# Weighed rows added to the output one step sooner, scatters issued ahead of the additions, experts' numbers read ahead: a graph layer and a mixture of experts on one core

## The chip, the cores and the metric

The kernel runs on one core of one Trainium2 chip. The metric is the device time of one execution in microseconds; smaller is better. The core has five engines with an instruction queue each: TensorE (PE, with its weight loads shown apart as PEld), VectorE (DVE), ScalarE (ACT), GpSimd (POOL) and SyncE (SP). Each queue works in order. In this kernel SP issues the plain transfers (rows of the profile marked SPq), and POOL issues the indirect ones (gathers, scatters, and additions into rows of the output). A transfer is issued by one instruction and lands some microseconds later; what needs it waits for the landing.

## The reference, cut to what matters

```python
x = x + gnn(layernorm(x), edges)          # 6250 nodes, 512 features, 106250 edges
x = x + ffn(layernorm(x))                 # a mixture of 8 experts, the best 2 for each token

def ffn(t):
    logits = gelu(t @ Wg1 + bg1) @ Wg2 + bg2
    topv, topi = top_k(softmax(logits), 2)
    topv = topv / sum(topv)
    cw = sum(one_hot(topi, 8) * topv[..., None], axis=1)     # a token's weight for each expert
    h = einsum('td,edh->eth', t, W1) + b1                    # 512 -> 256
    h = gelu(ln(h, g1, be1))
    h = einsum('eth,ehg->etg', h, W2) + b2                   # 256 -> 256
    h = gelu(ln(h, g2, be2))
    o = einsum('eth,eho->eto', h, W3) + b3                   # 256 -> 512
    return einsum('te,eto->to', cw, o)
```

The graph part (mean over neighbours, two products, batch norm) comes first and isn't touched by the change. The expert part is computed for the two chosen experts of each token alone.

## The kernel before, in words

**First part.** Until about 1200 us the kernel gathers neighbours' rows and multiplies; until about 1320 us it normalizes the first two groups of tokens.

**Second part.** The 6250 tokens form 49 tiles of 128 in 7 groups of 7 tiles. A tile of tokens is loaded, normalized and added to its input (`token_load`, `token_mul`, `token_add`, `token_sum` and others); `token_sum` (L843) writes the tile into `out` by an SP transfer (L844, called the store below). The routing of a group (`route`) then finds for each token its two experts and a row in `xs_d`, a table in DRAM ordered by expert, and `send` scatters the group's rows there: two indirect transfers of 128 rows per tile of tokens (`row_scatter`, L877).

A job is one tile of 128 rows of `xs_d` that all belong to one expert; 102 jobs run. A job goes through a pipeline of steps written out in `run(s, ...)`: step s works on job s in its first stage, on job s-1 in its second, and so on. With lag in steps: 0 transpose the rows on PE (`job_turn`), 1 first product (`layer`, L1103), 2 normalize (`layer_norm`, L806), 3 transpose and gelu (`layer_turn`), 4 second product, 5 and 6 the same again, 7 third product (`job_product`, L1132), 8 add the bias on DVE (`job_bias`, L1139) and multiply by the tokens' weights on ACT (`job_weigh`, L1143), 9 add the 128 rows into `out` by an indirect accumulating transfer on POOL (`job_out`, L1147, called the addition below). Job p+3 is loaded by SP in step p (`job_load`, L1082: the 512 features into `xe`, and weights and row numbers into `ev`).

**What sets the order.** There is no scheduler here: each engine's queue holds the instructions in the order in which `run` writes them. While tokens are still to be moved, a step also carries one tile of tokens through its own stages, and lists `do` and `late` of the step hold parts of the routing and the scatters. On POOL a step of before therefore reads: the addition of job s-9, then two scatters where the step has any, then the power that turns variances into scales (L797, called the power below). The power of step s ends the step: `shifts` of the next step (DVE L801) waits for it, and the normalizations on ACT wait for that.

**Dependences that matter here.** The additions are chained: each waits for the landing of the one before, because two jobs can hold the same token. Each also waits for the landing of every store of `out` that stands ahead of it in the program, and for its own weighing. A load of `xe` waits for the landing of all scatters ahead of it in the program. `oe` has three buffers, `ev` fourteen, so `job_bias` and the load of `ev` wait for additions of earlier jobs.

An expert's number lies in memory and must be brought into a register of each engine that picks weights by it (`values_load` in `job_turn`, L1088, on PE, DVE and ACT, at the start of the step).

Of the kernel before, what the change touches and what calls it, by code (L numbers as in the profile page):

```python
# [10 lines left out]
I32 = mybir.dt.int32  # L11
# [17 lines left out]
def gnn_moe_kernel(ctx: ExitStack, tc: tile.TileContext, x, src, dst, wlT, b_l, wrT, gamma, beta,  # L29
                   wg1, bg1, wg2, bg2, w1, b1, g1T, be1T, w2, b2, g2T, be2T, w3, b3, out):  # L30
    nc = tc.nc
    N, D = x.shape
    NE = src.shape[0]
    E, _, H = w1.shape
# [33 lines left out]
    NQ = -(-NT // 7)  # L68
# [3 lines left out]
    SLOTS = (2 * N + E * (P - 1)) // P  # L72
# [26 lines left out]
    w3s = const.tile([P, KH, E, D], F32, name="w3s")  # L99
    b1s = const.tile([P, E, H], F32, name="b1s")  # L100
    b2s = const.tile([P, E, H], F32, name="b2s")
    b3s = const.tile([P, E, D], F32, name="b3s")

    gbe = const.tile([P, E, 4, KH], F32, name="gbe")
# [7 lines left out]
    expert = const.tile([P, E], F32, name="expert")  # L112
# [34 lines left out]
    with ExitStack() as gnn:  # L147
        big = gnn.enter_context(tc.tile_pool(name="big", bufs=1))
        edge = gnn.enter_context(tc.tile_pool(name="edge", bufs=1))
        first = ExitStack()  # L150
# [247 lines left out]
        XT, Z = {}, {}  # L398
# [375 lines left out]
    JOBS = {}  # L774
# [293 lines left out]
            send_one(q, j, i)  # L1068


    XE, EV, XT, HN, HT, OE = {}, {}, {}, {}, {}, {}
    PE_, DVE_, ACT_, SP_ = (mybir.EngineType.PE, mybir.EngineType.DVE, mybir.EngineType.Activation,
                            mybir.EngineType.SP)

    def job_load(p):
# [7 lines left out]
            tc.add_to_no_dep_group("full", ld.ins)  # L1083
        XE[p] = xe, ev

    def job_turn(p):
        xe, ev = XE.pop(p)
        e = nc.values_load(JOBS[p][1], engines=[PE_, DVE_, ACT_], min_val=0, max_val=E - 1,  # L1088
                           skip_runtime_bounds_check_because="an expert's number")
        EV[p] = e, ev[:, 0:1].bitcast(I32), ev[:, 1:1 + E][:, ds(e, 1)]  # L1090
        pt = ps.tile([P, KD, P], F32, name="pt", bufs=3)
        for k in range(KD):
            nc.tensor.transpose(pt[:, k, :], xe[:, k * P:(k + 1) * P], ident)
        XT[p] = sb.tile([P, KD, P], F32, name="xT")
        nc.scalar.copy(XT[p], pt)

    def layer(p, i, step):
        e = EV[p][0]
        lhs, w, b, kk = (XT, w1s, b1s, KD) if i == 0 else (HT, w2s, b2s, KH)
        lhs = lhs.pop(p)  # L1100
        pm = ps.tile([P, H], F32, name="pm", bufs=2)
        for k in range(kk):
            nc.tensor.matmul(pm, lhs[:, k, :], w[:, k, ds(e, 1), :].rearrange("p o h -> p (o h)"),  # L1103
                             start=(k == 0), stop=(k == kk - 1))
        hn = sb.tile([P, H], F32, name=f"hn{i}", bufs=3)
        nc.vector.tensor_add(hn, pm, b[:, ds(e, 1), :].rearrange("p o h -> p (o h)"))  # L1106
        HN[p] = hn, step.stats(1 + i, hn)

    def layer_norm(p):
# [3 lines left out]
    def layer_turn(p, i):  # L1113

        e = EV[p][0]
        hn, _ = HN.pop(p)
        hT = sb.tile([P, KH, P], F32, name=f"hT{i}")
        pt = ps.tile([P, KD, P], F32, name="pt", bufs=3)
        for k in range(KH):
            nc.tensor.transpose(pt[:, k, :], hn[:, k * P:(k + 1) * P], ident)  # L1120
        for k in range(KH):
            gb = gbe[:, ds(e, 1), :, k].rearrange("p o j -> p (o j)")
            nc.scalar.activation(hT[:, k, :], pt[:, k, :], AF.Gelu,  # L1123
                                 bias=gb[:, 2 * i + 1:2 * i + 2], scale=gb[:, 2 * i:2 * i + 1])
        HT[p] = hT

    def job_product(p):
        e = EV[p][0]
        hT = HT.pop(p)
        po = ps.tile([P, D], F32, name="po")  # L1130
        for k in range(KH):
            nc.tensor.matmul(po, hT[:, k, :], w3s[:, k, ds(e, 1), :].rearrange("p o h -> p (o h)"),  # L1132
                             start=(k == 0), stop=(k == KH - 1))
        OE[p] = po

    def job_bias(p):
        e = EV[p][0]
        oe = sb.tile([P, D], F32, name="oe", bufs=3)
        nc.vector.tensor_add(oe, OE[p], b3s[:, ds(e, 1), :].rearrange("p o h -> p (o h)"))  # L1139
        OE[p] = oe  # L1140

    def job_weigh(p):
        nc.scalar.mul(OE[p], OE[p], EV[p][2])  # L1143

    def job_out(p):
        _, to, _ = EV.pop(p)
        st = nc.gpsimd.indirect_dma_start(  # L1147
            out=out[:, :], out_offset=bass.IndirectOffsetOnAxis(ap=to[:, 0:1], axis=0),
            in_=OE.pop(p), in_offset=None, bounds_check=N - 1, oob_is_err=False, compute_op=OP.add)
        tc.add_to_no_dep_group("added", st.ins)  # L1150
# [7 lines left out]
    def at(lag):  # L1158
        return seq[-1 - lag] if lag < len(seq) else None

    def enter():

        nonlocal entered
        seq.append(flat[entered] if entered < let_in else None)
        entered += seq[-1] is not None
# [34 lines left out]

    MOST = SLOTS - 3

    def run(s, prev, lo, hi, moves=False, do=(), late=()):


        def on(lag):
            return lo <= s - lag < hi

        step = Step()
        if moves:  # L1210
            enter()
            if at(0):
                token_load(*at(0))
        loads(min(s + 4, hi))
        if on(0):
            job_turn(s)
        for i, lag in ((0, 3), (1, 6)):
            if on(lag):
                layer_turn(s - lag, i)
        if on(9):  # L1220
            job_out(s - 9)
        if on(8):
            job_bias(s - 8)
        if moves:
            if at(5):
                token_logits(*at(5))
            if at(1):
                token_mul(*at(1))
        tprev.shifts()
        prev.shifts()  # L1230
        if moves:
            if at(1):
                token_add(*at(1))
            if at(2):
                token_sum(*at(2), step)
        for lag in (2, 5):
            if on(lag):
                layer_norm(s - lag)
        if moves and at(3) and at(3) != normed_one:
            token_norm(*at(3))  # L1240
        if on(8):
            job_weigh(s - 8)
        if moves and at(1):
            token_shift(*at(1))
        for f in do:
            f()
        if on(1):
            layer(s - 1, 0, step)
        if on(4):
            layer(s - 4, 1, step)  # L1250
        if on(7):
            job_product(s - 7)
        for f in late:
            f()
        if moves and at(3):
            token_turn(*at(3))
        if moves and at(4):
            token_gate(*at(4))
        step.scales()
        return step  # L1260
# [20 lines left out]
    with tc.manual_schedule():  # L1281
# [26 lines left out]
        n = n0 + n1  # L1308
# [25 lines left out]
        prev = Step()  # L1334
        for q in range(NQ):
            lo = done[q - 1] if q else 0
            n = done[q] - lo
            do = [[] for _ in range(n)]
            late = [[] for _ in range(n)]
            if q + 1 < NQ:  # L1340

                g = len(groups[q + 1])

                def put(where, i, f, *args):
                    where[min(i, n - 1)].append(lambda: f(*args))


                r = int(q == 1)
                if q:
                    put(do, r, begin, q + 1)  # L1350
                    for where, i in ((do, 0), (do, 0), (late, 0), (do, 1), (do, 1), (do, 2), (do, 3)):
                        put(where, r + i, part, q + 1)
                    a, b, end = r + 4, r + 10, (11, 12)
                    if q + 2 == NQ:
                        a, b = 3, 9
                else:
                    for where, i in ((late, 0), (do, 1), (do, 1), (do, 2), (do, 2)):
                        put(where, i, part, 1)
                    a, b, end = 3, 5, (4, 5)
                for j in range(g):  # L1360
                    put(do, a + j * (b + 1 - a) // g, send, q + 1, j)
                if q + 2 < NQ:
                    put(do, end[0], part, q + 1)
                else:
                    for i in (4, 5, 6):
                        put(do, i, part, q + 1)
                    for e in range(E):
                        put(do, 10 + (3 * e + 1) // E, free_rows, e)
                put(do, end[1], listed_all, q + 1)
            for i in range(min(n, MOST - lo)):  # L1370
                if i == (3 if q else 0) and q + 2 < NQ:
                    let(q + 2)
                prev = run(lo + i, prev, 0, MOST, q + 1 < NQ, do[i], late[i])
                if q == NQ - 1 and i == 6:
                    flag = nc.values_load(more[0:1, 0:1], skip_runtime_bounds_check_because="it is 0 or 1")
        for s in range(MOST, MOST + 10):
            prev = run(s, prev, 0, MOST)
    with tc.If(flag > 0), tc.manual_schedule():
        prev = Step()
        for s in range(MOST, SLOTS + 10):  # L1380
            prev = run(s, prev, MOST, SLOTS)


# [35 lines left out]
```

## Time and profile before

| what | us |
|---|---|
| median of 14 runs | 2041.21 (2035.87 to 2047.15) |
| the profiled execution: its time | 2038.17 |
| the profiled execution: its span | 2036.4 |
| the additions L1147: 102 | 165.7 busy, 1624 ns each |
| the scatters L877 from tokens: 98 | 101.4 busy, 1034 ns each |
| the powers L797: 121 | 107.1 busy, 885 ns each |
| PE, DVE, ACT, POOL busy over the span | 1863.6, 1062.9, 646.6, 1224.3 |

The span is that of one profiled execution, from its first to its last instruction; 1.8 us lie around it. The profiled execution is 3.0 us quicker than the median. Times in timelines count from the start of the span. An engine's row gives the start, the duration, the source line and, in square brackets, how long the engine stood idle before it and what the profile takes for the end of that wait. Where the engine named there had long been done, it was something else, often the landing of a transfer.

### The profile page before, as it was taken

Reading aid. Unit: us, or ns where it says so; the run is one execution under the profiler, and the core shown is the slowest. Engines: PE = TensorE matmul, PEld = TensorE weight load, DVE = VectorE, ACT = ScalarE, POOL = GpSimd, SP = SyncE. Lnnn points to the kernel's source line nnn. Section 1 sums busy time; section 2 is a strip of 40 time slices with the busy share of each in tenths; the row PEclk is TensorE's granted clock in tenths of the full one; section 3 lists DMA queues with packets and bytes.
Section 4 is the critical chain, followed back from the end, with each engine's and each line's share of the span. In section 5 each row is a group of like instructions: output and inputs, shape, how many; then the busy total and the mean of one; then the engine's idle time right before and its main releaser. Section 6 shows DMA issues by size and latency. Waiting matters only on the chain. (4 is left out here: it accounts for less than half of the span.)

```text
span 2036.4 us, 24258 instructions
## 1 busy us (share of the span) xinstructions
PE 1863.6 (92%) x6268; PEld 1029.6 (51%) x6268; DVE 1062.9 (52%) x2374; ACT 646.6 (32%) x1263; POOL 1224.3 (60%) x1236
## 2 busy tenths in 40 slices
PE   6878999999999999999999995679989998999993
PEld 2433444444444444444444443456667676666761
DVE  5652434334443444344344426768777777765551
ACT  3420101101010001011010114456666667656662
POOL 1427777777777777777777751445554546474343
PEclk9988999999999999999999997689999999999997
DMA  7968878778788888889888755646676767565532
GB/s 250 302 211 274 255 239 256 240 239 250 242 242 267 267 260 275 260 273 312 269 273 278 242 181 182 224 154 174 170 199 153 199 143 195 115 155 121 95 59 35
DMA packets 197875, 434.12 MB, mean 213 GB/s; under 512 B 47172, under 2 KB 53326, under 8 KB 197314
## 3 DMA queue, kind: packets, MB, share of 16 engines
q0 software_dynamic: 91040, 274.90, 48.2%
q1 hardware_dynamic: 106294, 156.70, 23.4%
q8 instruction: 56, 0.92, 0.2%
q10 hardware_dynamic: 396, 0.87, 0.1%
q14 instruction: 89, 0.73, 0.1%
HBM read 331.22 MB, written 104.20 MB: 214 GB/s over the span
## 5 line engine op out<-in xcount | busy, mean ns | idle before, releaser
L636 POOL DMA_INDIRECT xg<-xn_d,scol x832 | 794.8, 955 | 260.7 <-issue 124.2
L643 PE MATMUL pa<-xg,sel 128*128 128x512 f32 x1664 | 789.6, 597 | 20.3 <-issue 18.5
L643 PEld LDWEIGHTS pa<-xg,sel 128*128 128x128 f32 x1664 | 306.6, 191 | 365.0 <-issue 348.3
L1147 POOL DMA_INDIRECT out<-oe,ev x102 | 165.7, 1624 | 203.0 <-ACT hT L1123 52.2
L1103 PE MATMUL pm<-w1s,xT 128*128 x816 | 202.5, 392 | 8.5 <-DVE hn L1106 8.3
L1132 PE MATMUL po<-w3s,hT 128*128 x408 | 197.6, 607 | 11.4 <-DVE oe L1139 11.4
L528 ACT ACTIVATE sq<-dt 128x512 f32<-128x512 f32 x49 | 29.5, 602 | 557.5 <-DVE dt L526 281.5
L562 DVE TENSOR_REDUCE ss<-sel 128x128 f32<-128x2304 f32 x49 | 200.5, 4091 | 0.3 <-issue 0.2
L432 PE MATMUL ph<-wl,xT 128*128 128x512 f32 x392 | 199.8, 592 | 0.7 <-ACT xT L427 0.7
L797 POOL TENSOR_TENSOR mv<-mv,mhalf 128x2 f32<-128x2 f32 (+2 forms) x121 | 107.1, 885 | 151.3 <-DVE mv L796 149.2
L1103 PEld LDWEIGHTS pm<-w1s,xT 128*128 128x128 f32 x816 | 150.2, 194 | 28.1 <-DVE hn L1106 10.5
L1123 ACT ACTIVATE hT<-pt,gbe 128x128 f32<-128x128 f32 x408 | 153.9, 461 | 1.6 <-PE pt L1120 1.6
L806 ACT ACTIVATE hn<-hn,mv 128x256 f32<-128x256 f32 x204 | 112.0, 599 | 132.4 <-DVE mv L801 132.1
L507 DVE TENSOR_SCALAR rc<-pt 128x1 f32<-128x1 f32 x49 | 7.7, 158 | 272.2 <-PE pt L586 272.2
L556 DVE TENSOR_TENSOR sel<-jrow_p,dcol 128x2304 f32<-128x2304 f32 x49 | 124.4, 2539 | 0.0
L877 POOL DMA_INDIRECT xs_d<-t,pos x98 | 101.4, 1034 | 36.6 <-issue 25.0
L432 PEld LDWEIGHTS ph<-wl,xT 128*128 128x128 f32 x392 | 74.4, 190 | 94.2 <-issue 93.2
L526 DVE TENSOR_TENSOR dt<-ph,shift 128x512 f32<-128x512 f32 x25 | 17.3, 692 | 192.4 <-PE ph L432 192.4
L1132 PEld LDWEIGHTS po<-w3s,hT 128*128 128x128 f32 x408 | 77.0, 193 | 75.0 <-issue 53.0
L567 ACT ACTIVATE ag<-pa,rc 128x512 f32<-128x512 f32 x49 | 33.7, 687 | 249.0 <-PE pa L643 249.0
L524 DVE TENSOR_TENSOR dt<-ph,xo 128x512 f32<-128x512 f32 x24 | 16.6, 691 | 182.3 <-PE ph L432 182.3
L1103 PE MATMUL pm<-w2s,hT 128*128 x408 | 106.3, 383 | 0.0
(302 smaller groups left out, 2205.3 us busy)
## 6 DMA issues: line engine op xcount, KB each, us to landing
xe<-xs_d SPq DMA_DIRECT2D x102, 256.0 KB
xg<-xn_d,scol POOLq DMA_INDIRECT x832, 3.9
d_d<-dt SPq DMA_DIRECT2D x49, 256.0 KB
dt<-d_d SPq DMA_DIRECT2D x49, 256.0 KB
xt<-in_x SPq DMA_DIRECT2D x24, 512.0 KB
xn_d<-xt SPq DMA_DIRECT2D x24, 512.0 KB
xy<-y_d SPq DMA_DIRECT2D x48, 256.0 KB
xt<-in_x SPq DMA_DIRECT2D x48, 256.0 KB
```

The source lines that it names most:

```text
L432: nc.tensor.matmul(p, xT[:, k, :], w[:, k, :], start=start and k == 0, stop=stop and k == KD - 1)
L556: nc.vector.tensor_tensor(SEL[t], jrow_p[:, None, :].to_broadcast([P, KS, P]), dcol[:, t // TG, (t % TG) * KS:(t % TG + 1) * KS, None].to_ ...
L562: nc.vector.tensor_reduce(ss, SEL[t].rearrange("p k j -> p j k"), AX.X, OP.add)
L636: nc.gpsimd.indirect_dma_start(out=xg, out_offset=None, in_=xn_d[:, :], in_offset=bass.IndirectOffsetOnAxis(ap=scol[:, t // TG, c:c + 1], ...
L643: nc.tensor.matmul(PA[t], SEL[t][:, k, :], xg, start=(k == 0), stop=(k == last))
L797: nc.gpsimd.tensor_tensor(self.part[:, :, 1], self.part[:, :, 1], mhalf[:, :hi - lo], op=OP.pow)
L806: nc.scalar.activation(out_, in_, AF.Identity, bias=scale_shift[1], scale=scale_shift[0])
L877: st = nc.gpsimd.indirect_dma_start(out=xs_d.rearrange("n p c -> (n p) c"), out_offset=bass.IndirectOffsetOnAxis(ap=at, axis=0), in_=rows_ ...
L1103: nc.tensor.matmul(pm, lhs[:, k, :], w[:, k, ds(e, 1), :].rearrange("p o h -> p (o h)"), start=(k == 0), stop=(k == kk - 1))
L1123: nc.scalar.activation(hT[:, k, :], pt[:, k, :], AF.Gelu, bias=gb[:, 2 * i + 1:2 * i + 2], scale=gb[:, 2 * i:2 * i + 1])
L1132: nc.tensor.matmul(po, hT[:, k, :], w3s[:, k, ds(e, 1), :].rearrange("p o h -> p (o h)"), start=(k == 0), stop=(k == KH - 1))
L1147: st = nc.gpsimd.indirect_dma_start(out=out[:, :], out_offset=bass.IndirectOffsetOnAxis(ap=to[:, 0:1], axis=0), in_=OE.pop(p), in_offset=N ...
```

## The change

Three things are moved; no arithmetic is changed.

1. `job_out` is called in the step in which its job is weighed (lag 8), right after `job_weigh`, and no longer at the start of the next step (lag 9). The loops over the last steps are shorter by one.
2. The scatters (`send`, `free_rows`) go into a list `first`, which `run` works off before `job_bias`, and no longer into `do`. On POOL a step now reads: scatters, the addition of job s-8, the power. In the stretch of the last group of scatters they are spread over steps 4 to 9 and no longer 3 to 9, so that step 4 has those of two tiles.
3. The experts' numbers for job s+1 are read in step s: on DVE behind `job_bias`, on ACT behind the weighing and the `do` list, on PE behind the first product. Each engine now has a register of its own.

```diff
+    def number(p, engine):
+        if p in JOBS and engine not in NUMBER.setdefault(p, {}):
+            NUMBER[p][engine] = nc.values_load(JOBS[p][1], engines=[engine], min_val=0, max_val=E - 1,
+                                               skip_runtime_bounds_check_because="an expert's number")
     def job_turn(p):
         xe, ev = XE.pop(p)
-        e = nc.values_load(JOBS[p][1], engines=[PE_, DVE_, ACT_], min_val=0, max_val=E - 1,
-                           skip_runtime_bounds_check_because="an expert's number")
+        for engine in (PE_, DVE_, ACT_):
+            number(p, engine)
+        e = NUMBER.pop(p)
...
-    def run(s, prev, lo, hi, moves=False, do=(), late=()):
+    def run(s, prev, lo, hi, moves=False, first=(), do=(), late=()):
...
-        if on(9):
-            job_out(s - 9)
+        for f in first:
+            f()
         if on(8):
             job_bias(s - 8)
+        if on(-1):
+            number(s + 1, DVE_)
         if moves:
...
         if on(8):
             job_weigh(s - 8)
+        if on(8):
+            job_out(s - 8)
         if moves and at(1):
             token_shift(*at(1))
         for f in do:
             f()
+        if on(-1):
+            number(s + 1, ACT_)
         if on(1):
             layer(s - 1, 0, step)
+        if on(-1):
+            number(s + 1, PE_)
         if on(4):
...
                     if q + 2 == NQ:
-                        a, b = 3, 9
+                        a, b = 4, 9
...
-                    put(do, a + j * (b + 1 - a) // g, send, q + 1, j)
+                    put(first, a + j * (b + 1 - a) // g, send, q + 1, j)
...
-                        put(do, 10 + (3 * e + 1) // E, free_rows, e)
+                        put(first, 10 + (3 * e + 1) // E, free_rows, e)
...
-        for s in range(MOST, MOST + 10):
+        for s in range(MOST, MOST + 9):
```

More of the change, by code (lines that the diff above doesn't have):

```diff
@@ L1068, in send @@
             send_one(q, j, i)
-    XE, EV, XT, HN, HT, OE = {}, {}, {}, {}, {}, {}
+    XE, EV, XT, HN, HT, OE, NUMBER = {}, {}, {}, {}, {}, {}, {}
     PE_, DVE_, ACT_, SP_ = (mybir.EngineType.PE, mybir.EngineType.DVE, mybir.EngineType.Activation,
@@ L1084, in job_load @@
         XE[p] = xe, ev
+    def number(p, engine):
+        if p in JOBS and engine not in NUMBER.setdefault(p, {}):
+            NUMBER[p][engine] = nc.values_load(JOBS[p][1], engines=[engine], min_val=0, max_val=E - 1,
+                                               skip_runtime_bounds_check_because="an expert's number")
     def job_turn(p):
         xe, ev = XE.pop(p)
-        e = nc.values_load(JOBS[p][1], engines=[PE_, DVE_, ACT_], min_val=0, max_val=E - 1,
-                           skip_runtime_bounds_check_because="an expert's number")
-        EV[p] = e, ev[:, 0:1].bitcast(I32), ev[:, 1:1 + E][:, ds(e, 1)]
+        for engine in (PE_, DVE_, ACT_):
+            number(p, engine)
+        e = NUMBER.pop(p)
+        EV[p] = e, ev[:, 0:1].bitcast(I32), ev[:, 1:1 + E][:, ds(e[ACT_], 1)]
         pt = ps.tile([P, KD, P], F32, name="pt", bufs=3)
@@ L1102, in layer @@
         for k in range(kk):
-            nc.tensor.matmul(pm, lhs[:, k, :], w[:, k, ds(e, 1), :].rearrange("p o h -> p (o h)"),
+            nc.tensor.matmul(pm, lhs[:, k, :], w[:, k, ds(e[PE_], 1), :].rearrange("p o h -> p (o h)"),
                              start=(k == 0), stop=(k == kk - 1))
         hn = sb.tile([P, H], F32, name=f"hn{i}", bufs=3)
-        nc.vector.tensor_add(hn, pm, b[:, ds(e, 1), :].rearrange("p o h -> p (o h)"))
+        nc.vector.tensor_add(hn, pm, b[:, ds(e[DVE_], 1), :].rearrange("p o h -> p (o h)"))
         HN[p] = hn, step.stats(1 + i, hn)
@@ L1121, in layer_turn @@
         for k in range(KH):
-            gb = gbe[:, ds(e, 1), :, k].rearrange("p o j -> p (o j)")
+            gb = gbe[:, ds(e[ACT_], 1), :, k].rearrange("p o j -> p (o j)")
             nc.scalar.activation(hT[:, k, :], pt[:, k, :], AF.Gelu,
@@ L1131, in job_product @@
         for k in range(KH):
-            nc.tensor.matmul(po, hT[:, k, :], w3s[:, k, ds(e, 1), :].rearrange("p o h -> p (o h)"),
+            nc.tensor.matmul(po, hT[:, k, :], w3s[:, k, ds(e[PE_], 1), :].rearrange("p o h -> p (o h)"),
                              start=(k == 0), stop=(k == KH - 1))
@@ L1138, in job_bias @@
         oe = sb.tile([P, D], F32, name="oe", bufs=3)
-        nc.vector.tensor_add(oe, OE[p], b3s[:, ds(e, 1), :].rearrange("p o h -> p (o h)"))
+        nc.vector.tensor_add(oe, OE[p], b3s[:, ds(e[DVE_], 1), :].rearrange("p o h -> p (o h)"))
         OE[p] = oe
@@ L1337, in gnn_moe_kernel @@
             n = done[q] - lo
+            first = [[] for _ in range(n)]
             do = [[] for _ in range(n)]
@@ L1372, in gnn_moe_kernel @@
                     let(q + 2)
-                prev = run(lo + i, prev, 0, MOST, q + 1 < NQ, do[i], late[i])
+                prev = run(lo + i, prev, 0, MOST, q + 1 < NQ, first[i], do[i], late[i])
                 if q == NQ - 1 and i == 6:
                     flag = nc.values_load(more[0:1, 0:1], skip_runtime_bounds_check_because="it is 0 or 1")
-        for s in range(MOST, MOST + 10):
+        for s in range(MOST, MOST + 9):
             prev = run(s, prev, 0, MOST)
@@ L1379, in gnn_moe_kernel @@
         prev = Step()
-        for s in range(MOST, SLOTS + 10):
+        for s in range(MOST, SLOTS + 9):
             prev = run(s, prev, MOST, SLOTS)
```

## The prediction

> **What bounds the kernel now.** The page comes first. The chain that ended last holds only the final addition, so it says nothing of the rest. PE is busy for 92% of the span, the other engines for 32 to 60%:
>
> ```profile
> PE 1863.6 (92%) x6268; PEld 1029.6 (51%) x6268; DVE 1062.9 (52%) x2374; ACT 646.6 (32%) x1263; POOL 1224.3 (60%) x1236
> ```
>
> That is a mean over stages, and the change touches only those in which additions run (1379 us to the end). So I cut that part into stretches with the view of windows. Columns: window, length, then PE, PEld, DVE, ACT, POOL busy, granted clock, DMA share, GB/s.
>
> ```profile
> 1492.77:1539.19 46.42, 41.07 (x199) 28.81 (x198) 33.81 (x83) 33.55 (x68) 28.02 (x24) 0.96 0.77 217
> 1548.02:1591.13 43.11, 42.99 (x203) 30.84 (x204) 32.62 (x126) 28.08 (x61) 19.85 (x17) 1.00 0.64 137
> 1842.00:1888.00 46.00, 46.00 (x210) 34.54 (x209) 25.60 (x77) 32.00 (x72) 19.12 (x17) 0.98 0.59 111
> 1888.00:1965.00 77.00, 73.73 (x328) 52.07 (x328) 40.82 (x120) 47.81 (x107) 30.08 (x26) 1.00 0.51 87
> ```
>
> The second and third are filled by PE (42.99 of 43.11, 46.00 of 46.00): there only a later end of the additions can matter. The first is one of four spans of six steps that store a token tile; in it PE stands for 5.35 us though no engine is full. What holds it is read from the timelines of POOL, SP's queue and DVE, in that order (start, duration, line; in brackets the idle time before):
>
> ```profile
> 1500.25 1.77 POOL L1147 DMA_INDIRECT out<-oe,ev  x1 [1.55 <-DMA out<-xt]
> ...
> 1503.64 0.99 POOL L877 DMA_INDIRECT xs_d<-t,pos  x1 [0.31 <-issue]
> 1504.78 0.88 POOL L797 TENSOR_TENSOR mv<-mv,mhalf 128x3 f32<-128x3 f32 x1
> 1508.30 1.62 POOL L1147 DMA_INDIRECT out<-oe,ev  x1 [2.64 <-ACT t L806]
> ...
> 1512.53 0.94 POOL L797 TENSOR_TENSOR mv<-mv,mhalf 128x3 f32<-128x3 f32 x1
> 1518.31 1.62 POOL L1147 DMA_INDIRECT out<-oe,ev  x1 [4.84 <-ACT gts L866]
> ```
>
> ```profile
> 1502.19 0.34 SPq L1082 DMA_DIRECT2D xe<-xs_d  x1
> ...
> 1503.24 0.44 SPq L844 DMA_DIRECT2D out<-xt  x1
> ...
> 1509.63 0.34 SPq L1082 DMA_DIRECT2D xe<-xs_d  x1
> ...
> 1510.68 0.43 SPq L844 DMA_DIRECT2D out<-xt  x1
> ```
>
> ```profile
> 1513.50 0.17 DVE L801 SCALAR_TENSOR_TENSOR mv<-mv 128x3 f32<-128x3 f32 x1 [0.99 <-POOL mv L797]
> ...
> 1514.18 0.68 DVE L843 SCALAR_TENSOR_TENSOR xt<-dt,xt 128x512 f32<-128x512 f32 x1
> ```
>
> POOL stands ahead of the additions for 1.55, 2.64 and 4.84 us, and the power that ends the step is queued behind them. The ACT work named is long over; it is the landing of the store (in the trace's semaphore records the store of 1503.24 lands at 1507.49, and 0.81 later the addition starts). The store stood behind a load of `xe`, which waited for the scatters of the step before. So here the limit is a circle over two steps: scatter, 5.9 to landing, load, 1.05, store, 4.25, 0.81, addition, scatters, power. The four spans are 44.35, 46.42, 46.04 and 44.95 long (from the end of one power to that of the sixth after): 181.76/24 = 7.57 us a step.
>
> **The change part by part.**
>
> *Addition into the step of its store.* It goes ahead of the power of its own step, but program order keeps it behind the store of that same step, which in before had until the next step. The circle now closes in one step: end of a power, `shifts`, L828 and L843 (1513.47 to 1514.86: 1.40), the store, its landing L, 0.81, then addition and power (1.62 + 0.95 = 2.57): 4.78 + L. Against 7.57 this breaks even at L = 2.8. What L will be is the open price, and the 28 stores of before give rows by what stands about them. Nothing near: 2.05 and 2.02 (1399.53, 1442.14). A load of `xe` 1.04 ahead, scatters only behind: 2.77 and 2.58 (1437.17, 1631.74). Scatters 2.75 and 4.07 ahead, no load: 2.87 and 3.19 (1540.02, 1638.01). Load 1.04 ahead, scatters within 1.5, an addition 1.7 to 3.2 ahead whose transfer is still under way: 3.95 to 4.73, twice above 6 (most of the 24). In after the addition stands 2.57 + 1.40 = 3.97 ahead of the next store, the scatters 1.1 ahead and 0.2 behind it. The load is held by the scatters of the step before; these land 1.6 + 5.9 = 7.5 after a power's end, so about as the next power ends, and the load goes out some 1.4 ahead of the store. Nearest in this order is the store of 1716.38 (addition 4.54, scatters 2.47 and 1.14, load 1.04 ahead): 3.96; with the load's part gone the two of 2.87 and 3.19. I take the mean of these three, L = 3.34: 8.12 a step, (8.12 - 7.57) x 24 = **+13**. Low end: L = 2.0 gives 6.8, about PE's own 41.07/6 = 6.85, so -17. High end: L = 4.25 gives 9.03, so +35.
>
> One store is of another kind, the last tile's with 106 rows (1734.90): it took 6.62 to land. Its step becomes 1.40 + 6.62 + 0.81 + 2.57 = 11.4 against the 8.8 that DVE set for it: **+2.6** (0 if a full queue made the 6.62, +4 if a load adds to it).
>
> *Scatters ahead.* On POOL they move into time in which it waits for the addition's releasers. In the six-step spans this is in the sum above. In the first scatter step of a group nothing is stored; there POOL ran an addition (start 1487.78), two scatters, the power, and another addition. Two scatters cost 2 x 1.32 behind the addition; ahead of it about 1 us of the step was POOL's alone. Three later groups: **-3** (0 to -6). SP's load waits for the scatters' landing and they now issue 1.9 us earlier in the step. In the last group step 4 gets two tiles' scatters: 0.3 + 4 x 1.32 + 2.36 = 7.95 against 7.89, nothing (-3 to +3). In these steps the cover is PE.
>
> *The end.* From 1842 the additions' chain is the limit, each behind the landing of the one before: 1842.47 to 2026.26, 33 intervals of 5.57. They run behind PE's 5.18 a step until 1888, then the powers are tied to them:
>
> ```profile
> 1863.02 0.72 POOL L797 TENSOR_TENSOR mv<-mv,mhalf 128x2 f32<-128x2 f32 x1 [2.16 <-DVE mv L796]
> 1864.93 1.59 POOL L1147 DMA_INDIRECT out<-oe,ev  x1 [1.19 <-ACT hT L1123]
> ...
> 1898.64 1.59 POOL L1147 DMA_INDIRECT out<-oe,ev  x1 [3.40 <-ACT oe L1143]
> 1899.71 1.29 POOL L797 TENSOR_TENSOR mv<-mv,mhalf 128x2 f32<-128x2 f32 x1
> ```
>
> Taken one step sooner, the addition no longer starts 0.20 after a power's end (1848.39) but 2.36 before it (1898.64 to 1901.00): a head start of about 2.5. In the tied part (1888 to 1965) an interval is 5.99, in the free part 5.57; there SP's loads wait for the additions' landing (31 waits, 79.0 us in SP's queue over the last 790 us) and then run beside the next one. With a step's more room they need not: 13 x 0.42 = 5.5, of which I take half. But the tie also begins sooner, at 1842: 8 x 0.42 = +3.4 against. Taken **-5**; ends -8 and +1.
>
> *Numbers read ahead.* A read takes 0.30 on PE, 0.31 on DVE and 0.28 on ACT (102 each). None lies between the end of a power and the store. PE's gaps ahead of its work do not change where the read stands; DVE's idle time ahead of `job_bias` is 50.7 over all jobs, but what it waits for is late for other reasons. **0** (-2 to +2); the cover is the wait for the power, and without it 102 x 0.3 would be 31.
>
> *Sum:* 13 + 2.6 - 3 - 5 = +8. The profiled execution took 2038.17 (span 2036.4 + 1.8), 3.0 less than the median; the stretches are differences within it, so I add them to the median: 2041.2 + 8 = 2049.
>
> *Rules beside the rows.* The Trainium skill, "DMA: Bandwidth & Descriptors" (anatomy of one DMA, SWDGE path), gives about 2.0 us plus bytes over 436 GB/s, by estimate 2.6 us for this store of 256 KB; the step would be 7.4, the term -4 and the sum 2032. That fit is for POOL's kind of queue; the rows above hold 2.0 as well as 4.25. The same page (issuing engines are not separate DMA queues) says that all queues interleave on the same 16 engines. It speaks against this change: scatters put ahead still share the engines with the store that everything now waits for. The 0.77 share in the first window shows them far from empty.
>
> **The rivals.**
>
> 1. *The store lands early* (the other side). Place: the same 24 steps. If the load of `xe` gets well ahead and the previous addition's transfer is over when the store starts, L is that of stores with one neighbour, 2.6 to 2.8, or of clear ones: 2.6 gives 7.38 and -5, 2.3 gives 7.08 and -12; with the others (2.6 - 3 - 5 = -5) that is -10 to -17, 2024 to 2031. It decides from L = 2.85 (a term of +1.4, a sum of -4). For it: the addition is 1.5 further from the store than in most rows. Against: scatters start within 1.1 of every store, and the DMA share is already 0.77.
> 2. *The store lands as late as before.* With L = 4.25 the term is +35, at 3.9 +27: 2063 to 2071. For it: most of the 24 had it so, and two took over 6; PE's waits get longer, and its granted clock is 0.89 and 0.96 in two of the spans already. Against: a slower step gives the load a longer lead, which shortens L.
> 3. *It does nothing.* The chain of additions sets the end and takes up what the steps lose, and the tie's later intervals give back the head start: 2037 to 2043. Against: jobs must be produced before they are added, and 24 slower steps delay all of them.
>
> **How the numbers follow.** Forecast (L 3.1 to 3.6, 2043 to 2055): 0.38. Rival 1: 0.30. Rival 2: 0.18. Rival 3: 0.14. Changes under 0.2%, 4.1 us, cannot be told from none. Faster by more: rival 1 and a little of rival 3: 0.32. Same: the most of rival 3 and the foot of the forecast: 0.17. Slower: 0.51. Cases of both signs hold much of the chance, so the range takes in rival 1 but for its far end and the nearer part of rival 2: 2026 to 2066; the forecast's own is 2043 to 2055.
>
> **What would show it.** In the after profile: stores of the six-step spans that land after 3.1 to 3.6, powers 8.1 apart; the step at about 1735 over 11 us; the additions at the end still 5.6 to 6 apart. Powers 7.3 apart or less mean rival 1, 8.7 or more rival 2. I am wrong if the load of `xe` still stands 1.05 ahead of the store, if a gain lies in the steps filled by PE, or if the reads matter.

## The result and the profile after

The changed kernel takes 2059.05 us (median of 13 runs, 2052.71 to 2065.4) against 2039.73 for the kernel before (62 runs): a ratio of 1.0092, 95% interval 1.0078 to 1.0105, some 19 us slower. The forecast was 2049. The side was right, but the forecast had less than half of the amount.

The profiled execution has a span of 2057.9 us, 21.5 more than before. On the page the work is the same, and spread over a longer time (engine, busy time, share of the span, instructions):

```profile
PE 1861.7 (90%) x6268; PEld 1023.8 (50%) x6268; DVE 1063.3 (52%) x2374; ACT 646.7 (31%) x1263; POOL 1237.6 (60%) x1236
```

The windows of the changed kernel that answer to the first two shown of before, and two of the end (window, length, busy PE, PEld, DVE, ACT, POOL, granted clock, DMA share, GB/s):

```profile
1499.96:1549.05 49.09, 40.24 (x202) 27.97 (x201) 33.34 (x83) 33.35 (x68) 31.67 (x24) 1.00 0.78 207
1557.88:1601.00 43.12, 42.60 (x200) 30.23 (x200) 32.74 (x125) 28.10 (x61) 20.42 (x17) 1.00 0.61 138
1875.03:1924.97 49.94, 49.64 (x221) 35.17 (x220) 27.85 (x81) 32.40 (x72) 21.29 (x18) 1.00 0.57 97
1924.97:1991.44 66.47, 65.72 (x289) 45.87 (x288) 37.11 (x108) 42.88 (x96) 28.37 (x25) 1.00 0.50 85
```

The six steps with stores take 49.09 for 46.42, with PE idle for 8.85 of them though its clock was granted in full; the stretch filled by PE takes 43.12 for 43.11. So the loss lies where the tiles are stored. There POOL's timeline (start, duration, in brackets the idle time before) shows the new order, with the addition ahead of each power:

```profile
1513.69 1.94 POOL L1154 DMA_INDIRECT out<-oe,ev  x1 [2.44 <-DVE oe L1146]
1515.09 1.47 POOL L797 TENSOR_TENSOR mv<-mv,mhalf 128x3 f32<-128x3 f32 x1
1516.76 1.53 POOL L877 DMA_INDIRECT xs_d<-t,pos  x1 [0.19 <-issue]
1518.59 0.98 POOL L877 DMA_INDIRECT xs_d<-t,pos  x1 [0.30 <-issue]
1522.17 1.89 POOL L1154 DMA_INDIRECT out<-oe,ev  x1 [2.60 <-DVE oe L1146]
1523.51 1.47 POOL L797 TENSOR_TENSOR mv<-mv,mhalf 128x3 f32<-128x3 f32 x1
```

SP's queue over the same step:

```profile
1515.61 0.34 SPq L1082 DMA_DIRECT2D xe<-xs_d  x1
...
1517.99 0.35 SPq L844 DMA_DIRECT2D out<-xt  x1
```

And DVE, which the power lets go:

```profile
1516.60 0.17 DVE L801 SCALAR_TENSOR_TENSOR mv<-mv 128x3 f32<-128x3 f32 x1 [2.41 <-POOL mv L797]
1516.67 0.69 DVE L828 TENSOR_TENSOR dt<-dt,bn_b 128x512 f32<-128x512 f32 x1
1517.28 0.68 DVE L843 SCALAR_TENSOR_TENSOR xt<-dt,xt 128x512 f32<-128x512 f32 x1
```

The circle closes in one step, as its parts say: the power ends at 1516.56, the store goes out at 1517.99 (1.43 later), lands at 1521.38 by the semaphore records (3.39), the addition starts at 1522.17 (0.79), and the power behind it ends at 1524.98 (2.81). That is 8.42. The bracket blames DVE, but the `job_bias` that ended at 1521.89 is that of the next job. This addition's own bias was added by 1513.59 and its rows were weighed on ACT by 1519.21:

```profile
1512.90 0.69 DVE L1146 TENSOR_TENSOR oe<-po,b3s 128x512 f32<-128x512 f32 x1
...
1518.50 0.71 ACT L1150 ACTIVATE oe<-oe,ev 128x512 f32<-128x512 f32 x1
```

The addition before it had landed too, 2.1 or more ahead in each of the 24 steps with stores. What is left is the landing of the store: in 23 of the 24 the addition starts 0.79 to 0.88 after it.

The groups of waits from 1250 us on say the same from the other side. Before the change and after it, the time in which DVE's `shifts` waited for the power (us in total, times, longest):

```profile
DVE mv L801 <- POOL mv L797: 82.8, 46, 4.3
```

```profile
DVE mv L801 <- POOL mv L797: 182.3, 100, 5.1
```

**Where the 21 us went.** The ends of the powers mark the steps in both kernels (121 of them, one a step). Numbering them from 0, the 24 token steps end with the powers 27 to 32, 41 to 46, 55 to 60 and 69 to 74. Times in us, each worked out as a difference of two such marks; "end" is the start of the last addition.

| stretch | before | after | difference |
|---|---|---|---|
| power 20 to 26 | 37.7 | 37.9 | +0.2 |
| the 24 token steps | 181.8 (7.57 each) | 201.5 (8.39 each) | +19.7 |
| the step of the last tile's store (74 to 75) | 8.8 | 10.8 | +2.0 |
| the 31 other steps up to power 82 | 199.6 | 202.8 | +3.3 |
| power 82 to the end | 239.2 | 234.7 | -4.5 |
| power 20 to the end | 666.9 | 687.7 | +20.7 |

### The profile page after: what moved, and what is told of

Read it like the earlier page. It is cut to its first block, busy times and chain, and to the rows that moved or that the text cites. A ratio compares the mean times of both kernels' runs of the same rounds, so it can differ in the third digit from the quotient of the medians.

```text
span 2057.9 us, 24256 instructions
## 1 busy us (share of the span) xinstructions
PE 1861.7 (90%) x6268; PEld 1023.8 (50%) x6268; DVE 1063.3 (52%) x2374; ACT 646.7 (31%) x1263; POOL 1237.6 (60%) x1236
## 5 line engine op out<-in xcount | busy, mean ns | idle before, releaser
L797 POOL TENSOR_TENSOR mv<-mv,mhalf 128x2 f32<-128x2 f32 (+2 forms) x121 | 140.3, 1160 | 75.9 <-DVE mv L796 71.3
L877 POOL DMA_INDIRECT xs_d<-t,pos x98 | 113.9, 1162 | 31.9 <-issue 24.6
L801 DVE SCALAR_TENSOR_TENSOR mv<-mv 128x2 f32<-128x2 f32 (+2 forms) x121 | 19.6, 162 | 182.4 <-POOL mv L797 182.3
```

What stands on the lines that cost most here:

```text
L797: nc.gpsimd.tensor_tensor(self.part[:, :, 1], self.part[:, :, 1], mhalf[:, :hi - lo], op=OP.pow)
L877: st = nc.gpsimd.indirect_dma_start(out=xs_d.rearrange("n p c -> (n p) c"), out_offset=bass.IndirectOffsetOnAxis(ap=at, axis=0), in_=rows_ ...
```

## The experiments

In these runs every kernel, that of before too, took some 200 us more than in the profiles shown so far. Their traces show why this does not matter here: the extra time lies ahead of the additions (power 10 ends at 1463 to 1486 us, and at 1287 and 1288 in the first two profiles). So two things are read of each experiment: the ratio to the kernel before that ran beside it, and the marks of the table above, which start after that stage. The changed kernel, unaltered, was run again as e8.

> The changed kernel again, unaltered, beside the others on their chip: 15 to 22 us over the kernel before.

It came to 687.3 from power 20 to the end, against 687.7 in the first profile, with token steps of 8.34. Its ratio was 1.0052 (1.0014 to 1.0090), some 12 us and less than the 15 to 22 expected. The stage ahead of the additions alone scatters by 20 us in these runs, so the marks are the sharper measure. They hold to about 2 us over the whole part (e4, in which the reads alone differ from the kernel before, needs 669.1 for 666.9) and less well over a stretch of it (from power 82 on 243.1 for 239.2). The ratios put every experiment lower against the kernel before than the marks do, by 4 to 16 us (e1: 34 under it by the ratio, 18.5 by the marks). What is left over lies outside the part that the marks measure, and its cause stayed open.

| kernel | ratio (95%) | token step | 31 other steps and 74 to 75 | power 82 to end | power 20 to end |
|---|---|---|---|---|---|
| before (first profile) | | 7.57 | 208.4 | 239.2 | 666.9 |
| after (first profile) | 1.0092 (1.0078-1.0105) | 8.39 | 213.7 | 234.7 | 687.7 |
| e1, store behind the addition | 0.9847 (0.9799-0.9895) | 6.73 | 214.5 | 234.8 | 648.4 |
| e2, scatters first only | 0.9869 (0.9827-0.9910) | 6.67 | 208.3 | 244.9 | 651.2 |
| e3, addition only | 1.0485 (1.0424-1.0546) | 11.39 | 226.6 | 246.9 | 787.3 |
| e4, numbers only | 0.9992 (0.9968-1.0017) | 7.56 | 207.4 | 243.1 | 669.1 |
| e5, turn at the last group's jobs | 0.9882 (0.9813-0.9952) | 6.70 | 206.8 | 240.4 | 647.3 |
| e6, after with two stores | 1.0158 (1.0076-1.0241) | 8.81 | 223.1 | 235.6 | 707.0 |
| e7, e1 with two stores | 0.9925 (0.9889-0.9962) | 6.97 | 215.8 | 234.5 | 655.1 |
| e8, after again | 1.0052 (1.0014-1.0090) | 8.34 | 214.6 | 235.3 | 687.3 |

**e1: the store behind the addition in program order.** The wait of the addition for its own step's store goes, and nothing else is moved: the store still goes out at the same place in SP's queue.

```diff
         nc.vector.scalar_tensor_tensor(xt, dt, 0.0, xt, op0=OP.max, op1=OP.add)
-        w = nc.sync.dma_start(out[t * P:t * P + r, :], xt[:r])
-        tc.declare_no_dep(w.ins, group="added", reason="rows that no expert has seen yet")
+        def store():
+            w = nc.sync.dma_start(out[t * P:t * P + r, :], xt[:r])
+            tc.declare_no_dep(w.ins, group="added", reason="rows that no expert has seen yet")
         tokens[q, j] = xt, step.stats(0, xt)
+        return store
...
         if on(8):
             job_out(s - 8)
+        if store:
+            store()
```

> The changed kernel, with the store of the token tile put behind the addition of the same step in program order, so that the addition no longer waits for that store's landing; nothing else moves. Theory (the landing of the step's own store, with addition and power behind it, makes the step 8.3 us): the 24 token steps fall from 8.39 to about 7.0, close to what PE fills, so 24 x 1.4 = 33 less than the changed kernel: 2022 to 2034. Rival A (scatters ahead share the DMA engines with store and load, and that makes the steps long): the scatters stand where they stood, so 2052 to 2062. Rival B (the reads ahead cost): unchanged too, 2055 to 2062.

Token steps of 6.73 for 8.39, and 39 us less than the changed kernel by the marks: the theory stands, its 33 was a little short, and both rivals fall, since scatters and reads stand where they stood. It is faster than the kernel before as well: 0.9847. One of its steps on POOL:

```profile
1697.40 0.98 POOL L879 DMA_INDIRECT xs_d<-t,pos  x1 [0.30 <-issue]
1699.29 1.57 POOL L1156 DMA_INDIRECT out<-oe,ev  x1 [0.90 <-ACT tt L859]
1700.46 1.33 POOL L797 TENSOR_TENSOR mv<-mv,mhalf 128x3 f32<-128x3 f32 x1
```

and SP's store of that step, which the addition passes 1.15 after it was issued and 2.79 before it landed (1702.08 by the semaphore records):

```profile
1698.14 0.64 SPq L845 DMA_DIRECT2D out<-xt  x1
```

**e2: only the scatters ahead.** The addition stays a step behind its weighing, but behind the scatters.

```diff
-        if on(9):
+        for f in first:
+            f()
+        if on(9):
             job_out(s - 9)
```

with `first` filled as in the change, and no number read ahead.

> The kernel before, with only the scatters moved ahead of the addition (which stays a step behind its weighing, but now stands behind the scatters on POOL); no number is read ahead. Theory: the addition waits for the store of the step before, landed long ago, and the scatters no longer wait for it, so the loads go out earlier: token steps of 7.0 for 7.57, 24 x 0.57 = 14 less than before, 2022 to 2032. Rival A (scatters ahead are what costs): 2050 to 2060.

Token steps of 6.67, 0.9869. So of the three parts the moved scatters are a gain, 21.8 us in the token steps where 14 were expected; the earlier addition on top of them turns it into a loss. On POOL the scatters start 0.2 after a power's end, where in the kernel before they stood behind the waiting addition, 4.2 after it in the mean:

```profile
1672.89 1.11 POOL L877 DMA_INDIRECT xs_d<-t,pos  x1 [0.19 <-issue]
1674.31 0.98 POOL L877 DMA_INDIRECT xs_d<-t,pos  x1 [0.30 <-issue]
1676.93 1.57 POOL L1147 DMA_INDIRECT out<-oe,ev  x1 [1.64 <-ACT tt L857]
1678.11 1.32 POOL L797 TENSOR_TENSOR mv<-mv,mhalf 128x3 f32<-128x3 f32 x1
```

The views of windows of e1 and of e2, one token span each, show how full the engines are now:

```profile
1675.90:1714.92 39.02, 36.69 (x189) 25.91 (x188) 33.64 (x83) 32.10 (x64) 29.24 (x25) 1.00 0.95 260
```

```profile
1666.62:1705.82 39.20, 37.59 (x186) 25.77 (x185) 33.18 (x84) 31.33 (x63) 28.51 (x25) 1.00 0.97 259
```

The DMA share has risen from 0.77 to 0.95 and 0.97 at 260 GB/s, with PE busy for 94 to 96% of the time: transfers and PE are near full together. The next wait shows too. In 14 of the 24 token steps of e1 and in 16 of those of e2 the addition starts within 0.92 of the landing of the addition before it (in 6 of the kernel before, in none of the changed one). So the chain of additions has largely taken the place of the circle.

**e3: only the addition moved.**

```diff
-        if on(9):
-            job_out(s - 9)
...
             job_weigh(s - 8)
+            job_out(s - 8)
...
         for f in do:
             f()
```

> The kernel before, with only the addition moved into the step of its weighing; the scatters follow it on POOL, ahead of the power; no number is read ahead. Theory: the wait for the store is the same as in the changed kernel, but two scatters of 1.3 now stand between the addition and the power; the store lands some 0.9 sooner, with no scatter beside it: 8.39 + 2.64 - 0.9 = 10.1 a step, 24 x 2.5 = 61 more than before, less 3 at the end: 2085 to 2105. Rival A (scatters ahead are what costs): 2035 to 2042. Rival B: 2035 to 2042.

Steps of 11.39, 4.85% slower; the scatters ahead are thus what keeps the change from being far worse. By the marks it is 120 us over the kernel before, where 58 were expected. Some 29 of these lie outside the token steps, where nothing was expected but a small gain; 18 of the 29 are in the stretches between and behind them. The token steps themselves are 1.3 longer than expected, and POOL and SP say where:

```profile
1709.18 0.99 POOL L877 DMA_INDIRECT xs_d<-t,pos  x1 [0.31 <-issue]
1710.18 0.92 POOL L797 TENSOR_TENSOR mv<-mv,mhalf 128x3 f32<-128x3 f32 x1
1716.92 2.00 POOL L1147 DMA_INDIRECT out<-oe,ev  x1 [5.83 <-ACT hT L1123]
```

```profile
1712.27 0.34 SPq L1082 DMA_DIRECT2D xe<-xs_d  x1
...
1713.31 0.37 SPq L844 DMA_DIRECT2D out<-xt  x1
```

The store goes out 2.2 after the power's end (1711.10) and not 1.43: it stands behind the load, which goes out only when the late scatters have landed (the second at 1712.15 by the semaphore records, the load at 1712.27). Most of the rest lies in the store's landing, which was assumed at 2.3 and took 2.71 in the mean of the 24. It landed in 2.0 to 2.9 in 26 of the 28, quicker than with scatters beside it (3.36 in the mean), as assumed.

**e4: only the numbers read ahead** (the change with its other two parts undone).

> The kernel before, with only the experts' numbers read a step ahead. Theory: no read lies on the path of the power, 2038 to 2042. Rival B (a read of 0.3 behind the products holds PE, or one behind the addition of the bias holds DVE, 102 times): up to 2070. A gain would be at most 102 x 0.3 on PE where PE is full (some 70 steps): 2020 to 2038.

0.9992 (0.9968 to 1.0017), and 669.1 against 666.9 by the marks, within their scatter. The reads are neither gain nor loss that can be measured.

**e6 and e7: a second store of the same tile**, into a scratch tensor, ahead of the store of the output; e6 from the changed kernel, e7 from e1.

```diff
+        nc.sync.dma_start(twin_d[t * P:t * P + r, :], xt[:r])
         w = nc.sync.dma_start(out[t * P:t * P + r, :], xt[:r])
```

> The changed kernel, with the tile of every token step stored a second time, into a scratch tensor, just ahead of its store of the output: 256 KB more on SP's queue in front of it. Theory (a step is 5.1 us plus the landing of its store): the landing grows from 3.2 to about 4.0 and the step by the same, 9.1 to 9.3 us, 24 x 0.8 = 19 more than the changed kernel. Rival A (the step is set by POOL's own work and the scatters): 0 to 5 more.

> The kernel of e1 (the store behind the addition in program order), with the same second store. Theory: the landing is off the path of the power, so the token steps stay at 6.7 to 6.9, 0 to 5 more than e1. Rival (what the store costs is its traffic on the DMA engines): 10 to 19 more than e1.

e6 is 19.7 over e8 by the marks, as expected in sum but not in place: 11 in the token steps (8.81 for 8.34), 4 in the step of the last tile's store, 4 in the other steps between. The landing grew by only 0.2 (mean over the 24 stores 3.56 against 3.34 in e8), and the store goes out 0.37 later, behind the twin's issue; the step grew by 0.47 where 0.8 was expected. In e7 the token steps grow by 0.24 and the sum by 6.6, though its stores land later than those of e6 (4.27 in the mean). That 6.6 lies between the theory (0 to 5) and the rival (10 to 19). So more of what the second store costs in e6 is the path it lies on, and a part is its traffic. The pair points the same way as e1 without being as clean.

**e5: the addition a step behind, until the last group's jobs begin, and in its own step from there.**

```diff
+    TURN = done[NQ - 2]
...
-        if on(9):
+        if s <= TURN and on(9):
             job_out(s - 9)
...
             job_weigh(s - 8)
+            if s >= TURN:
+                job_out(s - 8)
```

> Scatters ahead of the addition, the addition one step behind its weighing (as in e2) until the last group's jobs begin, and in the step of its weighing from there on; no number read ahead. Theory: the place of the addition ahead of the power costs wherever stores, scatters or the routing run and gains only in the last steps. From the end of the 20th power after the first additions to the last addition: e2's 651 less the 5 to 12 by which the last steps of e1 are shorter, 639 to 646, so 21 to 28 less than the kernel before. Rival A (the early place is no gain in the last steps; their end is the chain's own): 648 to 654, 13 to 19 less.

647.3 is between the two expectations: not settled by the sum. From power 103 to the end it needs 112.2, with 111.8 in the changed kernel and 110.8 in e1, and 119.4 in e2 and 119.0 before: so the early place is worth some 7 us in the last steps. But the turn itself, a step with two additions, gives part of it back: that step takes 11.79 for e2's 6.91, and power 91 to 103 takes 74.5 for e2's 72.2. e1, e2 and e5 lie within 4 us of each other by the marks, and their intervals overlap; all three beat both kernels, and which of them is best was not settled.

## Why the prediction was off

The terms of the prediction add up to +7.6, and the marks give +20.7. Of the 13 between them 6.7 lie in the token steps, where the fixed part of the step was too small, and 6.3 in the other steps before the end, where -3 was put on the scatters and nothing on the earlier addition. The first is a size that was off, the second a step of the argument that failed.

*The addition into the step of its store: mechanism right, term mis-sized.* It said 4.78 + L. L was put at 3.34 from three stores of before and is 3.36 in the mean of the same 24 stores after. That it came so near is in part luck: the three rows were 2.87, 3.19 and 3.96, and the load of `xe`, put at 1.4 ahead of the store, stood 2.8 ahead of it (median). The rest was too small, 5.03 for 4.78. In the mean of the 24 steps the store went out 1.46 after the power for 1.40, the addition started 0.87 after the landing for 0.81, and the power ended 2.70 after the addition's start for 2.57. The 2.57 took the addition (1.62) and the power (0.95) from rows in which two scatters stood between them. Behind each other the power starts 1.0 to 1.5 after the addition and lasts 1.47. A quarter of a microsecond, 24 times, is 6 of the 6.7 by which +13 fell short of +19.7.

*The last tile's store:* +2.6 forecast, +2.0 measured (8.8 to 10.8). It landed after 6.64, but went out 0.83 after the power, where the sum had 1.40. A full queue is unlikely to have made the 6.62: this store of 106 rows takes 6.61 to 6.68 in six of the eight runs with one store a tile, e3 with its emptier queues among them (6.95 and 7.30 in the other two).

*Scatters ahead: the step that failed.* -3 was forecast in the first scatter step of each group. Those steps did get shorter (5.7 for 7.06, 7.61 and 6.86 in the three groups, 4.5 in all), but others got longer, and all together the 31 steps outside the token spans lost 3.3. One cause is the other part of the change, which the prediction left out of these steps. In before the power came in the gap between two additions; now each is behind one:

```profile
1478.08 1.59 POOL L1154 DMA_INDIRECT out<-oe,ev  x1 [2.22 <-ACT oe L1150]
...
1485.03 1.60 POOL L1154 DMA_INDIRECT out<-oe,ev  x1 [3.23 <-ACT xT L1102]
1486.35 1.06 POOL L797 TENSOR_TENSOR mv<-mv,mhalf 128x2 f32<-128x2 f32 x1
1491.92 1.59 POOL L1154 DMA_INDIRECT out<-oe,ev  x1 [4.52 <-ACT hT L1130]
1492.99 1.29 POOL L797 TENSOR_TENSOR mv<-mv,mhalf 128x2 f32<-128x2 f32 x1
```

Two additions are apart by the landing of the first and a little more (6.13 and 0.76 for that of 1485.03), and the step is as long as that wherever the landing is slow: 6.88 here, just ahead of the first scatter step, for 5.93 before (e2: 5.91). The experiments split it: with the addition a step behind, these stretches take 206.8 to 208.4 (before, e2, e4, e5), whether the scatters are ahead or not; with the addition in its own step 213.7 to 215.8 (after, e1, e7, e8). So with the addition a step behind, scatters ahead are worth nothing in sum, and the early addition costs 6, the last tile's step among it. With the early addition and the scatters behind it (e3) the same stretches take 226.6, so there scatters ahead save 13. That they save nothing in e2 has a second cause: its first scatter steps gain 4.9, but the second step behind each token span (to power 35, 49, 63 and 77) is longer by as much, 6.79 for 5.32 at the first. In the first three of these the power waits for DVE and not for an addition; what makes DVE late was not followed.

*The end:* -5 forecast, -4.5 measured, in part by luck. The prediction's own parts, 2.5 of head start and half of 5.5, with 3.4 against them, make -1.9; the -5 left the 3.4 out. Measured, power 82 to 103 lost 2.7 and the rest gained 7.2, so both the gain and what stood against it were there, and the gain was larger. Against e4, which has the end of the kernel before, the gain is 8. The step named is seen: the additions from 1889 to 1922 are 5.46 to 5.71 apart where those of before stood 5.99 apart in the tied part. Each power follows its addition 1.07 later:

```profile
1889.02 1.59 POOL L1154 DMA_INDIRECT out<-oe,ev  x1 [3.01 <-DVE mv L796]
1890.09 1.29 POOL L797 TENSOR_TENSOR mv<-mv,mhalf 128x2 f32<-128x2 f32 x1
1894.56 1.59 POOL L1154 DMA_INDIRECT out<-oe,ev  x1 [3.17 <-ACT hT L1130]
```

SP's wait for the additions' landing, from which the gain was argued, fell from 79.0 to 16.3 us. That the freed loads are the cause of the quicker landings was argued, not tried by itself.

*Numbers:* 0, as forecast (e4). DVE's idle time ahead of `job_bias` was given as 50.7; the view by line has 67.7 there. Nothing rested on it.

*The rivals.* The one on the other side (stores that land early) fell with L = 3.36; that of stores as late as before (4.25) too, and the chain of additions did not take up the loss. What the prediction did not see at all is that the scatters alone were a large gain: it put them into the sum of the token steps only together with the addition. In the circle of before that it drew, scatter, load, store, addition, scatter, it cut one edge and closed another, and never priced cutting the one alone.

By the Trainium skill's figure ("DMA: Bandwidth & Descriptors", anatomy of one DMA, SWDGE path) the landing was estimated at 2.6 us; the 24 stores of the changed kernel took 2.76 to 3.91, and 6.54 once. The rule of the same page (issuing engines are not separate DMA queues) that all queues share the same engines agrees with e3 against the changed kernel: 2.71 in the mean with no scatter beside the store, 3.36 with one. The load stands at another distance from the store in the two, so this is not a clean trial of it.

## What to carry to other kernels

An operation moved earlier keeps the waits that program order gives it: look for transfers that were a step old when it waited for them and are now its own step's, and for what is queued behind it on its engine. Where a wait is on a transfer issued by a third engine, putting that transfer behind the waiting operation in program order (where the data allow it) can be worth more than the move. And price each part of a change alone: here one part was worth -22 us in the token steps, the other +41 on top of it.

## What the hardware showed that was not expected

- In the changed kernel a power of three values a row right behind an addition on POOL lasts 1.46 to 1.49 and begins before the addition (1.6 to 2.1) is over; with POOL idle ahead of it, it lasts 0.88 to 0.89.
- In e1 and e2 the six-step spans ran at a DMA share of 0.86 to 0.97, 238 to 262 GB/s. The stores of full tiles took up to 5 us to land there, but for one in each, and the token steps were still 6.7. That one took over 10 us, and there a step was long (10.53 and 9.74); in e2 the addition of that step started 0.79 after that landing.
- At the same place in the last group one step, that to power 73 or 74, was longer than its neighbours in every kernel; in the changed one transfers of all queues landed late there (8.3 for an addition, 8.2 for a load, 6.5 for a store; a step of 11.24). Just ahead of it, in all ten runs, SP issues the load of the last tile's 106 rows, which takes 6.9 to 9.2 us to land where the median for tiles of 128 rows is 3.8 to 5.0; in the first two profiles the semaphore records show 3 updates for it, and 16 for the transfers of 128 rows around it. That this load is what holds the others up is likely, and was not tried.
- The same changed kernel differed by some 200 us between two occasions in the stage ahead of the additions, and by 0.4 us in 687 after it.
